# Three dense chunks instead of two, and indirect DMAs tied one by one to TensorE products, in a gated scan followed by a mixture of experts

## Chip, cores and metric

One core of a Trainium2 chip. The time is the device time of one execution in microseconds, median of several runs. The kernel works in float32, apart from a few small helper matrices in bfloat16.

## What is computed

4096 tokens (16 sequences of 256) of 128 channels pass through two residual layers. The first is a gated linear recurrence along each sequence, the second a mixture of 32 experts of which each token uses four.

```python
# layer 1, on layernorm(x)
it = sigmoid(x @ Wi.T + bi);  rt = sigmoid(x @ Wr.T + br)
at = exp(-8.0 * softplus(cap_lambda) * rt)
h  = scan(h = at * h + sqrt(1 - at**2) * (it * x))
x  = x + layernorm(h)
# layer 2, on layernorm(x)
scores  = sigmoid(x @ gate_w.T)
topk    = top_k(scores + e_bias, 4);  weights = scores[topk] / sum
out     = sum over e of weight_e * (silu(x @ w1[e]) * (x @ w3[e])) @ w2[e]     # 128 -> 96 -> 128
x  = x + layernorm(out)
```

## The kernel before

The tokens are cut into eight chunks of 512. Every chunk goes through `mix` (layer 1, router, choice of four experts). Then a chunk takes one of two ways through the experts.

A **dense** chunk (chunks 0 and 7, `DENSE`) computes all 32 experts for all its tokens and multiplies by a combine weight that is zero for experts not chosen. The 32 x 96 = 3072 hidden units are cut into 24 steps (`UB`) of 128. In each step (`dense`), TensorE makes three products, `dg`, `du` (line 990, with w1 and w3) and `dw` (the combine weight spread over the units, bfloat16), ACT applies silu (line 998), DVE multiplies twice (lines 1001 and 1007), and a fourth product (line 1011) adds the step into the accumulator `acc`. `finish` transposes, normalizes and stores the chunk.

A chunk that goes **by token** belongs to a group, `GROUPS`: chunks 1 to 3 and chunks 4 to 6. `send` scatters each token's row four times, once for each chosen expert, into a table in DRAM with a region for each expert: sixteen indirect DMAs a chunk, all from POOL (line 450). When the whole group is sent, `loads` (line 790, SP) brings blocks of 128 rows of one expert back, four blocks at a time, and `experts` runs them: transpose (`xT_ps`, line 806), w1 and w3 together (`gu`, 820), silu and multiply (826, 828), transpose (`aT_ps`, 836), w2 (`y_ps`, 850), and a store to a second table in DRAM (861). A group has `tokens * 4 / 128 + 31` blocks, so that every expert's last block has room: 79 for three chunks. When a group's last block is stored, `fetch` gathers each token's four result rows, again with sixteen indirect DMAs a chunk (line 928), weights and adds them on DVE (936 to 944), and `combine` normalizes, adds the residual and stores.

The order of the instructions on TensorE, DVE, ACT and SP is fixed when the program is built. Each piece of work is a generator that yields the engine that it needs next and a planned cost; `Order.run` plays the pieces against each other by cost, due time and buffer slots, and emits the instructions in that order. A piece that yields `POOL, 1.29 * K` is charged for four indirect DMAs at once. Expert blocks are due early on TensorE, and dense steps late, so that dense steps fill in. POOL issues the indirect DMAs in the order of emission.

`after(ins, others)` makes an instruction wait for other instructions. `apart` declares that the scatters don't collide with each other.

Of the kernel before, what the change touches and what calls it, by code (L numbers as in the profile page):

```python
# [18 lines left out]
P = 128  # L19
EPS = 1e-5  # L20
K = 4
GROUPS = ((1, 2, 3), (4, 5, 6))
DENSE = (0, 7)
MIXES = 6
TILES = 40
HELD = 4
# [2 lines left out]
PE, DVE, ACT, POOL, SP, TIME = "pe", "dve", "act", "pool", "sp", "time"  # L29
# [88 lines left out]
SOON = 0.3  # L118
STAY = 6.0
LEAD, STEP, PACE = 45.0, 20.6, 0.9  # L120
SLOT, UNTIL = "slot", "until"


@with_exitstack
def tile_gated_scan_then_moe(
# [28 lines left out]
    nc = tc.nc  # L154
# [6 lines left out]
    SEQS = CH // T  # L161
    NG = len(GROUPS)
    TG = [CH * len(chunks) for chunks in GROUPS]
    UB = E * I // P
    NB = [t * K // P + E - 1 for t in TG]
    NBM = max(NB)
    QB = 4
    RB = 3
    assert C == P and H == P and CH % T == 0 and E * I % P == 0 and 3 * E <= P
    assert sorted(sum(GROUPS, ()) + DENSE) == list(range(N // CH))  # L170

# [20 lines left out]
    def after(ins, others):  # L192

        for o in others:
            tc.add_manual_dep(
                ins.ins, o.ins.name,
                mybir.DependencyInfo(mybir.DependencyClass.Sync, mybir.DependencyReason.DATA),
                reason="rows in DRAM",
            )
# [225 lines left out]
    def apart(ins, key):  # L425

        tc.declare_no_dep(ins.ins, group=key, reason="rows of their own")
        tc.add_to_no_dep_group(key, ins.ins)
# [7 lines left out]
    def normalize(comb, pool, c):  # L436
# [2 lines left out]
        nc.vector.reciprocal(total, total)  # L439
        nc.vector.tensor_tensor(comb, comb, total.to_broadcast([P, TPC, E]), ALU.mult)  # L440

    def send(g, cg):

        c = GROUPS[g][cg]
        yield UNTIL, lambda: times["rows", c][0] if ("rows", c) in times else None
        _, rows, hn = times["rows", c]
        for j in range(TPC):
            yield POOL, 1.29 * K
            for k in range(K):
                ins = nc.gpsimd.indirect_dma_start(  # L450
                    out=rows_in[g],
                    out_offset=bass.IndirectOffsetOnAxis(ap=rows[:, j, k : k + 1], axis=0),
                    in_=hn[:, j, :], in_offset=None,
                )
                apart(ins, f"in_{g}")
                sent[g].append(ins)
        times["sent", g] = order.now
        yield TIME, 2.5
        give("hn", "w")
# [25 lines left out]
    def mix(c):  # L485

        g = next((g for g in range(NG) if c in GROUPS[g]), None)
        if g is not None:
            cg = GROUPS[g].index(c)
        yield UNTIL, lambda: 0.0 if c < MIXES else times.get(("mixed", c - MIXES))  # L490
# [266 lines left out]
    ended = [0] * NG  # L757
# [36 lines left out]
    def experts(g, q):  # L794

        nb, n_ = min(QB, NB[g] - q), f"{g}_{q}"
        yield UNTIL, lambda: times["xb", g, q][0] if ("xb", g, q) in times else None
        yield UNTIL, lambda: 0.0 if began[g] == q // QB else None
        yield SLOT, "blk", "w", "w", "w"
        began[g] += 1  # L800
        _, xb = times["xb", g, q]
        yield SLOT, "s", "ps"
        yield PE, 0.11 * nb
        pt = bank(f"xT_ps_{n_}")
        for b in range(nb):
            nc.tensor.transpose(pt[:, b * P : (b + 1) * P], xb[:, b, :], ident)  # L806
        give("xb", "w")
        yield ACT, 0.6
        xT = work.tile([P, QB * P], F32, tag="w", name=f"xT_{n_}")
        nc.scalar.copy(xT[:, : nb * P], pt[:, : nb * P])  # L810
        give("s", "ps")
        act = work.tile([P, QB, P], F32, tag="w", name=f"act_{n_}")[:, :, :I]
        for h in range(0, nb, 2):
            m = min(2, nb - h)
            yield SLOT, "s", "ps"
            yield PE, 0.33 * m
            pg = bank(f"gu_{n_}_{h}")[:, : 4 * I].rearrange("p (b f) -> p b f", b=2)
            for b in range(m):
                _, e = regs[g, q + h + b]
                nc.tensor.matmul(  # L820
                    pg[:, b, :], lhsT=xT[:, (h + b) * P : (h + b + 1) * P],
                    rhs=w13[:, :, bass.ds(e, 1), :].rearrange("h s o i -> h s (o i)"),
                    start=True, stop=True,
                )
            yield ACT, 0.33, "silu"
            nc.scalar.activation(act[:, h : h + m, :], pg[:, :m, 0:I], AF.Silu)  # L826
            yield DVE, 0.35
            nc.vector.tensor_tensor(  # L828
                act[:, h : h + m, :], act[:, h : h + m, :], pg[:, :m, I : 2 * I], ALU.mult
            )  # L830
            give("s", "ps")
        yield SLOT, "s", "ps"
        yield PE, 0.11 * nb
        pa = bank(f"aT_ps_{n_}")
        for b in range(nb):
            nc.tensor.transpose(pa[:I, b * P : (b + 1) * P], act[:, b, :], ident)  # L836
        aT = work.tile([P, QB * P], F32, tag="w", name=f"aT_{n_}")[:I]
        if q // QB % 2:
            yield DVE, 0.6
            nc.vector.tensor_copy(aT[:, : nb * P], pa[:I, : nb * P])  # L840
        else:
            yield ACT, 0.6
            nc.scalar.copy(aT[:, : nb * P], pa[:I, : nb * P])  # L843
        give("s", "ps")
        yield SLOT, "s", "ps"
        yield PE, 0.22 * nb
        py = bank(f"y_ps_{n_}").rearrange("p (b h) -> p b h", h=H)
        for b in range(nb):
            _, e = regs[g, q + b]
            nc.tensor.matmul(  # L850
                py[:, b, :], lhsT=aT[:, b * P : (b + 1) * P],
                rhs=w2_sb[:, bass.ds(e, 1), :].rearrange("i o h -> i (o h)"),
                start=True, stop=True,
            )
        yield SLOT, "yb", "w"
        yield ACT, 0.6
        yb = work.tile([P, QB, H], F32, tag="w", name=f"yb_{n_}")
        nc.scalar.copy(yb[:, :nb, :], py[:, :nb, :])  # L858
        give("s", "ps", "blk", "w", "w", "w")
        yield SP, 0.4  # L860
        done[g].append(nc.sync.dma_start(
            out=rows_out[g].rearrange("(i p) h -> p i h", p=P)[:, q : q + nb, :],
            in_=yb[:, :nb, :],
        ))
        ended[g] += 1
        if (q // QB + 1) % RB == 0 or q + QB >= NB[g]:
            give("regs")
        times["done", g] = order.now
        yield TIME, 2.5
        give("yb", "w")  # L870
# [46 lines left out]
    def fetch(g, cg, j):  # L917

        c = GROUPS[g][cg]
        yield UNTIL, lambda: times["done", g] + 2.5 if ended[g] * QB >= NB[g] else None  # L920
        yield UNTIL, lambda: times["slots", c][0] if ("slots", c) in times else None
        yield UNTIL, lambda: 0.0 if fetched[0] == turn[c] * TPC + j else None
        yield SLOT, "yk", "w"
        _, rows, wk = times["slots", c]
        yield POOL, 1.29 * K
        yk = work.tile([P, K, H], F32, tag="w", name=f"yk_{c}_{j}")
        for k in range(K):
            ins = nc.gpsimd.indirect_dma_start(  # L928
                out=yk[:, k, :], out_offset=None, in_=rows_out[g],
                in_offset=bass.IndirectOffsetOnAxis(ap=rows[:, j, k : k + 1], axis=0),  # L930
            )
            after(ins, done[g])
        fetched[0] += 1
        yield TIME, 2.4
        yield DVE, 0.7
        nc.vector.tensor_tensor(
            yk, yk, wk[:, j, :].unsqueeze(2).to_broadcast([P, K, H]), ALU.mult
        )
        yield DVE, 0.7
        nc.vector.tensor_tensor(yk[:, 0:2, :], yk[:, 0:2, :], yk[:, 2:4, :], ALU.add)  # L940
        yield UNTIL, lambda: times["res", c][0] if ("res", c) in times else None
        yield DVE, 0.4
        ff = times["res", c][1]
        nc.vector.tensor_tensor(ff[:, j, :], yk[:, 0, :], yk[:, 1, :], ALU.add)
        give("yk", "w")
        summed[c] = summed.get(c, 0) + 1
        times["summed", c] = order.now
# [19 lines left out]
    accs, acts = {}, {}  # L967
    downs = [0] * len(DENSE)

    def dense(d, k):  # L970

        c = DENSE[d]
        yield UNTIL, lambda: times["hT", c][0] if ("hT", c) in times else None
# [13 lines left out]

        def product(name, lhsT, rhs):
            ps = bank(f"d{name}_{c}_{k}")
            nc.tensor.matmul(ps, lhsT=lhsT, rhs=rhs, start=True, stop=True)  # L990
            return ps

        yield PE, 0.86
# [24 lines left out]
    def finish(d):  # L1018

        c = DENSE[d]  # L1020
        yield UNTIL, lambda: times["down", d] if downs[d] == UB else None
# [31 lines left out]
    for g, chunks in enumerate(GROUPS):  # L1053
# [15 lines left out]
        ]  # L1069
    for d, c in enumerate(DENSE):  # L1070
        pieces += [
# [36 lines left out]
```

## Time and profile before

| what | us |
|---|---|
| median of 3 runs | 440.73 (436.21 to 441.47) |
| the profiled execution's own time | 580.8 |
| its span, first to last instruction | 579.1 |
| mean granted TensorE clock in it | 0.823 of full speed |

| share of the chain that ended last | |
|---|---|
| PE | 48% |
| another core or an unknown queue | 16% |
| DVE | 13% |
| ACT | 11% |
| "issue" (no wait shown) | 11% |

The profile is of one execution, which took 140 us longer than the median of the others. A row of a group of instructions names the line, the engine, the operation, output and inputs, the count, then busy time and the mean of one in ns, and the idle time just before these instructions with what ended it. "remote" and "another core or an unknown queue" stand where the profile does not show who released the waiting engine. In the rows by slices the span is cut into 40 parts of 14.5 us, and each digit is the busy share in tenths.

### The profile page before, as it was taken

How to read it: one execution, taken by the hardware profiler on the slowest of the kernel's cores; microseconds unless marked ns; L12 is line 12 of the kernel's file. 1: busy time of each engine (PE TensorE's matmuls, PEld its weight loads, DVE VectorE, ACT ScalarE, POOL GpSimd, SP SyncE). 2: the span in 40 equal slices, each digit the busy share in tenths (PEclk: the TensorE clock that was granted, in tenths of full speed). 3: DMA queues.
4: the chain of work that ended last, by engine and by line, in shares of the span. 5: the costliest groups of instructions: out<-in, count | busy, mean ns of one | idle time of the engine just before them, and what ended most of it. 6: DMA issues, size and time to landing. Idle time of an engine off the chain costs nothing.

```text
span 579.1 us, 6527 instructions
## 1 busy us (share of the span) xinstructions
PE 368.5 (64%) x1555; PEld 236.8 (41%) x1555; DVE 313.5 (54%) x1185; ACT 251.6 (43%) x473; POOL 202.9 (35%) x227
## 2 busy tenths in 40 slices
PE   0345766767883982588559863288799993235940
PEld 0123342332432871477447542266678631012410
DVE  6956692839482763287218640257577451013785
ACT  1599895659421741666235311144355520001321
POOL 9200046643645017100720077236400077771000
PEclk9986767779698887699759985599899998666995
DMA  8245535100131133223222432044544212110001
GB/s 236 66 133 140 139 91 152 41 32 25 50 100 64 55 101 100 73 70 109 91 70 59 119 109 71 25 120 132 146 118 139 88 45 54 53 51 14 18 1 54
DMA packets 82068, 48.57 MB, mean 84 GB/s; under 512 B 15696, under 2 KB 78960, under 8 KB 82032
## 3 DMA queue, kind: packets, MB, share of 16 engines
q1 hardware_dynamic: 74976, 35.40, 21.6%
q0 software_dynamic: 6144, 12.60, 7.5%
q10 hardware_dynamic: 912, 0.17, 0.2%
q8 instruction: 13, 0.21, 0.1%
q14 instruction: 23, 0.19, 0.1%
HBM read 25.20 MB, written 22.94 MB: 83 GB/s over the span
## 4 chain that ended last, share of the span: by engine, by line
PE 48%; another core or an unknown queue 16%; DVE 13%; ACT 11%; issue 11%; DMA 1%; ACTq 0%; DVEq 0%
PE gu L820 9%; PE acc L1011 8%; PE y_ps L850 7%; PE dg L990 6%; PE du L990 6%; PE aT_ps L836 3%; PE xT_ps L806 2%; PE pl L569 2%; PE dw L990 1%; PE pi L510 1%; PE pr L510 1%; ACT h L395 1%; DVE nt_a L375 1%; DVE st_a L471 1%
## 5 line engine op out<-in xcount | busy, mean ns | idle before, releaser
L450 POOL DMA_INDIRECT rows_in<-hn,rows x96 | 92.7, 965 | 184.3 <-DVE x_all L551 60.6
L928 POOL DMA_INDIRECT yk<-rows_out,slots x96 | 93.1, 970 | 135.4 <-PE dw L990 50.1
L820 PE MATMUL gu<-w,xT 128*128 x316 | 71.3, 360 | 36.9 <-ACT xT L810 19.0
L1011 PE MATMUL acc<-a,w_all 128*128 128x512 f32 x96 | 58.4, 698 | 48.2 <-DVE a L1007 28.5
L820 PEld LDWEIGHTS gu<-w,xT 128*128 128x128 f32 x316 | 56.8, 210 | 45.9 <-issue 23.3
L998 ACT ACTIVATE a<-dg 128x512 f32<-128x512 f32 x48 | 28.6, 598 | 92.8 <-remote 38.6
L1007 DVE TENSOR_TENSOR a<-a,dw 128x512 f32<-128x512 f32 x48 | 32.4, 684 | 64.3 <-remote 34.9
L850 PE MATMUL y_ps<-w_sb,aT 96*128 x316 | 48.7, 305 | 26.2 <-ACT aT L843 11.3
L828 DVE TENSOR_TENSOR act<-act,gu 128x192 f32<-128x192 f32 x80 | 27.0, 346 | 67.9 <-ACT act L826 53.1
L850 PEld LDWEIGHTS y_ps<-w_sb,aT 96*128 96x128 f32 x316 | 43.8, 212 | 39.9 <-ACT aT L843 16.3
L826 ACT ACTIVATE act<-gu 128x192 f32<-128x192 f32 x80 | 25.7, 330 | 68.7 <-PE gu L820 29.7
L990 PE MATMUL dg<-hT,w 128*128 128x512 f32 x96 | 55.4, 662 | 0.0
L990 PE MATMUL du<-hT,w 128*128 128x512 f32 x96 | 50.9, 612 | 0.0
L858 ACT COPY yb<-y_ps 128x512 f32<-128x512 f32 (+1 forms) x40 | 23.1, 581 | 52.5 <-PE y_ps L850 23.4
L1001 DVE TENSOR_TENSOR a<-a,du 128x512 f32<-128x512 f32 x48 | 32.4, 681 | 23.6 <-issue 7.4
L1011 PEld LDWEIGHTS acc<-a,w_all 128*128 128x128 f32 x96 | 17.0, 211 | 67.9 <-DVE a L1007 40.3
L810 ACT COPY xT<-xT_ps 128x512 f32<-128x512 f32 (+1 forms) x40 | 22.8, 582 | 33.5 <-remote 23.8
L836 PE MATMUL aT_ps<-ident,act 128*96 128x128 f32 x158 | 25.6, 287 | 11.1 <-issue 7.4
L990 PEld LDWEIGHTS dg<-hT,w 128*128 128x128 f32 x96 | 20.2, 217 | 19.0 <-issue 17.6
L836 PEld LDWEIGHTS aT_ps<-ident,act 128*96 128x96 f32 x158 | 18.5, 132 | 19.4 <-issue 15.5
L806 PE MATMUL xT_ps<-ident,xb 128*128 128x128 f32 x158 | 25.4, 297 | 0.4 <-DVE lists L749 0.4
L990 PEld LDWEIGHTS du<-hT,w 128*128 128x128 f32 x96 | 18.7, 205 | 14.6 <-issue 13.0
(205 smaller groups left out, 590.2 us busy)
## 6 DMA issues: line engine op xcount, KB each, us to landing
xb<-rows_in SPq DMA_DIRECT2D x158, 64.0 KB
rows_out<-yb SPq DMA_DIRECT2D x38, 256.0 KB
rows_in<-zeros SPq DMA_DIRECT2D x8, 512.0 KB
w<-in_L_ffn_w_dram SPq DMA_DIRECT2D x8, 384.0 KB
x_all<-in_L_attn_x_dram SPq DMA_DIRECT2D x8, 256.0 KB
w_all<-in_L_ffn_w_dram SPq DMA_DIRECT2D x4, 384.0 KB
w_sb<-in_L_ffn_w_dram SPq DMA_DIRECT2D x4, 384.0 KB
rows_in<-hn,rows POOLq DMA_INDIRECT x96
```

The source lines that it names most:

```text
L450: ins = nc.gpsimd.indirect_dma_start(out=rows_in[g], out_offset=bass.IndirectOffsetOnAxis(ap=rows[:, j, k : k + 1], axis=0), in_=hn[:, j, ...
L806: nc.tensor.transpose(pt[:, b * P : (b + 1) * P], xb[:, b, :], ident)
L820: nc.tensor.matmul(pg[:, b, :], lhsT=xT[:, (h + b) * P : (h + b + 1) * P], rhs=w13[:, :, bass.ds(e, 1), :].rearrange("h s o i -> h s (o i) ...
L828: nc.vector.tensor_tensor(act[:, h : h + m, :], act[:, h : h + m, :], pg[:, :m, I : 2 * I], ALU.mult)
L836: nc.tensor.transpose(pa[:I, b * P : (b + 1) * P], act[:, b, :], ident)
L850: nc.tensor.matmul(py[:, b, :], lhsT=aT[:, b * P : (b + 1) * P], rhs=w2_sb[:, bass.ds(e, 1), :].rearrange("i o h -> i (o h)"), start=True, ...
L928: ins = nc.gpsimd.indirect_dma_start(out=yk[:, k, :], out_offset=None, in_=rows_out[g], in_offset=bass.IndirectOffsetOnAxis(ap=rows[:, j, ...
L990: nc.tensor.matmul(ps, lhsT=lhsT, rhs=rhs, start=True, stop=True)
L998: nc.scalar.activation(a, pg, AF.Silu)
L1001: nc.vector.tensor_tensor(a, a, pu, ALU.mult)
L1007: nc.vector.tensor_tensor(a, a, pw, ALU.mult)
L1011: nc.tensor.matmul(accs[d], lhsT=w2_all[:, k, :], rhs=a, start=(k == 0), stop=(k == UB - 1))
```

## The change

The second group becomes chunks 4 and 5, and chunk 6 joins the dense chunks. The planner charges each indirect DMA by itself, at `RATE` = 1.9 instead of four at once at 1.29 each. And each indirect DMA waits for the last `y_ps`, `dg`, `du` or `dw` product that was emitted before it (`beat`). A gather is spaced and made to wait in this way only while dense steps or expert blocks are left to emit (`left`); after that it is charged 1.26 and waits as before. The `acc` product is not recorded in `beat`.

```diff
-GROUPS = ((1, 2, 3), (4, 5, 6))
-DENSE = (0, 7)
+GROUPS = ((1,2,3),(4,5))
+DENSE = (0,6,7)
...
+RATE = 1.9
...
+    beat = [None]
+
+    def in_pace(ins):
+
+        if beat[0] is not None:
+            after(ins, beat)
+
+    def left():
+
+        return sum(downs) < len(DENSE) * UB or any(ended[g] * QB < NB[g] for g in range(NG))
...
         for j in range(TPC):
-            yield POOL, 1.29 * K
             for k in range(K):
+                yield POOL, RATE
                 ins = nc.gpsimd.indirect_dma_start(
...
                 apart(ins, f"in_{g}")
+                in_pace(ins)
                 sent[g].append(ins)
...
-            nc.tensor.matmul(
+            beat[0] = nc.tensor.matmul(
                 py[:, b, :], lhsT=aT[:, b * P : (b + 1) * P],
...
-        yield POOL, 1.29 * K
         yk = work.tile([P, K, H], F32, tag="w", name=f"yk_{c}_{j}")
         for k in range(K):
+            yield POOL, RATE if left() else 1.26
             ins = nc.gpsimd.indirect_dma_start(
...
             after(ins, done[g])
+            if left():
+                in_pace(ins)
...
-            nc.tensor.matmul(ps, lhsT=lhsT, rhs=rhs, start=True, stop=True)
+            beat[0] = nc.tensor.matmul(ps, lhsT=lhsT, rhs=rhs, start=True, stop=True)
```

## The prediction

> **What bounds the kernel now.** I read the header and the rows by slices first, then the groups of instructions, then a table of three stretches, then the timeline inside a run of indirect DMAs and inside an undisturbed stretch.
>
> ```profile
> span 579.1 us, 6527 instructions
> PE 368.5 (64%) x1555; PEld 236.8 (41%) x1555; DVE 313.5 (54%) x1185; ACT 251.6 (43%) x473; POOL 202.9 (35%) x227
> ...
> PE   0345766767883982588559863288799993235940
> ...
> POOL 9200046643645017100720077236400077771000
> PEclk9986767779698887699759985599899998666995
> ...
> L450 POOL DMA_INDIRECT rows_in<-hn,rows x96 | 92.7, 965 | 184.3 <-DVE x_all L551 60.6
> L928 POOL DMA_INDIRECT yk<-rows_out,slots x96 | 93.1, 970 | 135.4 <-PE dw L990 50.1
> ```
>
> TensorE is busiest. It falls to 2 and 3 tenths where POOL stands at 6 to 7 tenths (slices 23 and 24, 34 to 36), and the granted clock falls with it. The 192 indirect DMAs are POOL's only work after the start.
>
> ```profile
> 28.00:172.00 144.00, 98.13 (x282) 49.74 (x283) 92.37 (x417) 105.04 (x169) 51.93 (x54) 0.77 0.32 90
> 172.00:460.00 288.00, 204.68 (x1135) 161.78 (x1134) 146.91 (x524) 118.78 (x253) 88.11 (x91) 0.85 0.32 93
> 460.00:579.00 119.00, 59.07 (x129) 22.87 (x127) 51.62 (x148) 17.45 (x35) 45.72 (x48) 0.77 0.14 37
> ```
>
> The columns are the stretch, its length, busy time of PE, PEld, DVE, ACT and POOL, then clock, DMA share and GB/s. I cut at the first block of an expert (172) and after the last one (460). Stage one is mixing, with ACT busy 105 of 144 us. Stage two is experts with dense steps between them. Stage three is the last 48 gathers beside the rest of the dense steps, and PE works only half of it. Why, the timeline of stage three shows:
>
> ```profile
> 504.92 0.94 POOL L928 DMA_INDIRECT yk<-rows_out,slots  x1 [0.30 <-issue]
> 505.17 0.60 ACT L998 ACTIVATE a<-dg 128x512 f32<-128x512 f32 x1 [18.37 <-remote]
> 506.17 0.95 POOL L928 DMA_INDIRECT yk<-rows_out,slots  x1 [0.30 <-issue]
> ...
> 509.31 0.69 DVE L1007 TENSOR_TENSOR a<-a,dw 128x512 f32<-128x512 f32 x1 [13.38 <-remote]
> ```
>
> The indirect DMAs go every 1.25 us without a gap, while ACT and DVE sit 18.37 and 13.38 us for products that PE had started by 493.95; the releaser is unknown. From 463.4 to 523.5 PE is idle 32 us by the timeline. Runs of four DMAs (5 us, around 390 and 396) show next to no such idleness. So the stall is real in this execution and belongs to long runs: PE's idle time inside runs after 165, beyond a normal tenth, comes to about 75 us; stage two and three also lose some 35 us to matmuls at the lower clock (busy time times one minus clock).
>
> **How this execution stands to the timed runs.** It took 580.8 us (span 579.1 and 1.7 around it); the median of three runs is 440.73. [...] Here it is 140 us. [...] 580.8 less about 110 us of stalls and clock leaves 471, still above 440.73. A timed run has room for few of them. I take the measurement, and this decides the sign.
>
> **What the change costs in dense steps.** One more chunk keeps all experts: 24 more steps (72 for 48). The undisturbed end gives the price:
>
> ```profile
> 550.33 1.12 PE L1011 MATMUL acc<-a,w_all 128*128 128x512 f32 x2
> ...
> 552.37 1.02 PE L990 MATMUL du<-hT,w 128*128 128x512 f32 x2
> ...
> 553.31 1.13 PE L1011 MATMUL acc<-a,w_all 128*128 128x512 f32 x2
> ```
>
> Start to start 2.98 us at full clock (where dg, du, acc and dw follow one another with no wait, 538.70 to 541.49, it is 2.79). So 24 x 2.98 = +71.5 us of PE. DVE gets 24 x (0.681 + 0.684) = 32.8 us and ACT 24 x 0.598 = 14.4, which lie under the step's 2.98 us of PE.
>
> **What it saves in blocks.** The second group loses a chunk: 512 tokens x 4 / 128 = 16 blocks (63 for 79). A block costs:
>
> ```profile
> 446.69 1.06 PE L850 MATMUL y_ps<-w_sb,aT 96*128 x8
> ...
> 447.58 0.82 PE L820 MATMUL gu<-w,xT 128*128 x4
> ...
> 449.00 1.02 PE L990 MATMUL dg<-hT,w 128*128 128x512 f32 x2
> ...
> 449.86 0.60 PE L836 MATMUL aT_ps<-ident,act 128*96 128x128 f32 x4
> ...
> 450.29 0.82 PE L820 MATMUL gu<-w,xT 128*128 x4
> ```
>
> y: 0.89 us for four blocks, gu about 0.65 for two, aT 0.43 for four, xT as aT: 0.22 + 0.325 + 0.11 + 0.11 = 0.76 us. 16 x 0.76 = -12.2 us of PE. Net on PE: +59. The 16 loads and four stores of those blocks leave SP's queue, and 32 of 192 indirect DMAs leave POOL (32 x 1.26 = 40 us); both engines were waiting, so this counts only where a run of gathers sets the end, below.
>
> **Where it lands.** The static order of the changed program, counted on PE: before the first block 20 dense steps are done (14 before the change), before the last block's product 33 (29), after it 39 (19). With the prices above, PE work up to the last block is about the same in both, 237 against 240 us; between first and last block it is 147 against 171. So the added work lies behind the last block.
>
> Stage three before, without stalls: first gather 3.7 us after the last product, 48 x 1.25 = 60.0, about 2 to land (assumed; no row), and 10.3 from the last yk multiply (568.75) to the end (579.1): 76 us. It covered its 19 dense steps (57 us). After: 39 x 2.98 = 116.2, and 11.6 from the last acc (555.44) to the end of a dense chunk (DVE's final add is at 562.91, the output as behind the last one): 128 us, or 120 at 2.79 a step. The 32 gathers, now spaced at the planner's 1.9 us, take 61 and hide. [...] Stage three: **+44 to +52**, taken +50.
>
> Stage one: each scatter now waits for the latest product emitted before it, so a chunk's 16 take about 16 x 1.9 = 30 us for 20. Behind the waiting scatter stand all later ones on POOL; the block loads on SP wait for the group's last. The third chunk's scatters began at 137.5 and ended at 157.5; now 168 to 170. **+11**; bounds: 0 if the products are done anyway, +30 if they lag. PE fills part of it with six more dense steps, which are already taken off stage three.
>
> Stage two: PE needs 24 us less. A timed run has about 440.7 - 165 - 76 = 200 us there for 171 of PE work (165 estimated from the 172 less the 5 to 7 us of stalls seen in stage one): 86%. At the same share 147 us takes 171, **-29**; at 92%, because the few real stalls go, 160, **-40**. Taken -34.
>
> Sum on the timed run: 440.7 + 11 - 34 + 50 = **468 us**. On the profiled execution: 580.8 + 11, less about 115 in stage two (stalls, clock, blocks), + 9 in stage three (128 for 119): about 485. So the profile should improve by far more than 50 us while the timed runs get slower.
>
> **Rivals.**
> Faster: the timed runs do lose time at long runs of indirect DMAs, only less than the profiled one. For: the link of run length to idleness. Against: the sum above. With 60 us of such losses removed, 468 becomes 408; PE's full-rate work (345) plus 28 us before it starts and 12 behind it make 385 a floor. It decides from about 45 us of losses. 405 to 431.
> No change: stage one ends earlier than I think (150 instead of 165), so stage two holds idleness that tighter spacing removes: 15 more us gained, and the scatter delay does not show: 468 - 15 - 11 = 442.
> Much slower: the waits on products lag the plan; the scatters of each chunk take 2.9 us apiece, the first block comes 30 us later, and dense chunk 0 has no steps left to cover it: about 490.
> The spacing may also do nothing, when products are always done before POOL asks. Then the profile keeps its stalls and the timed run lacks the 11 us and some of the 34: about 463, inside my own range.
>
> **Chances.** Forecast 0.69 (450 to 485), no change 0.15 (432 to 449), faster 0.11, much slower 0.05. A measurement of this kernel tells about 2% from no change (432 to 450). Faster 0.11, same 0.15, slower 0.74. The likeliest is 468; the range 441 to 488 leaves out the faster case and part of the last.
>
> **What the changed profile would show.** 72 steps in L990's groups; 142 blocks; the stretch behind the last y_ps about 128 us with PE over 90% busy at full clock; indirect DMAs 1.9 us or more apart, and no "remote" waits of 10 us. I am wrong if the stretch behind the last block is below 100 us, if it comes before 300 in a run as fast as the timed one, or if the timed runs drop along with the profiled one.

## The result, and the profile after

Timed side by side on one chip, the changed kernel took 484.43 us (median of 4 runs), the kernel before 439.39: a ratio of 1.104 (95% interval 1.096 to 1.113), slower. The profiled execution of the changed kernel has a span of 482.7 us.

The page of the changed kernel, its header and its rows by slices (12.1 us each):

```profile
span 482.7 us, 6679 instructions
PE 393.4 (81%) x1627; PEld 233.2 (48%) x1627; DVE 332.0 (69%) x1194; ACT 258.4 (54%) x481; POOL 172.6 (36%) x195
...
PE   1344475889798979899798888889999999998991
...
POOL 9400003455446464454100013544544545443100
PEclk9966775999789999999899999999999999998996
```

TensorE now works in 7 to 9 tenths of every slice after the first quarter but the last, and mostly at 9 tenths of its clock (0.932 in the mean). POOL never fills a slice by more than 6 tenths after the start. The holes of before are gone from the profile, and yet the timed result is 45 us worse.

Every expert block starts with its transpose (`xT_ps`) and ends with its last product (`y_ps`). In the changed kernel (duration min/median/max in ns, then first and last start in us):

```profile
L819 PE MATMUL xT_ps<-ident,xb x142: 270/273/333, 177.3 to 346.1; 128*128 128x128 f32 x142
...
L863 PE MATMUL y_ps<-w_sb,aT x284: 272/275/422, 186.6 to 355.6; 96*128 x142
```

Three stretches of it, from 28 us on, cut at the first block of an expert and after the last one (columns: stretch, length, busy time of PE, PEld, DVE, ACT, POOL, clock, DMA share, GB/s):

```profile
28.00:177.00 149.00, 113.17 (x354) 54.19 (x355) 113.94 (x504) 115.14 (x186) 51.96 (x53) 0.84 0.29 83
177.00:356.00 179.00, 160.28 (x989) 130.08 (x988) 108.39 (x365) 100.15 (x215) 58.73 (x61) 0.98 0.44 126
356.00:482.00 126.00, 113.56 (x277) 46.51 (x275) 86.85 (x230) 32.52 (x65) 44.71 (x47) 0.96 0.15 40
```

Stage three is 127 us long (to the end of the span) with PE busy 90% of it, against 119 us half idle in the profile of before. Part of the changed kernel's timeline in that stage:

```profile
424.67 1.02 PE L1005 MATMUL du<-hT,w 128*128 128x512 f32 x2
...
425.96 0.94 POOL L941 DMA_INDIRECT yk<-rows_out,slots  x1 [0.99 <-PE du L1005]
...
427.65 0.38 PE L1005 MATMUL dw<-combT,spread 96*128 96x512 bf16 x1
...
428.08 0.94 POOL L941 DMA_INDIRECT yk<-rows_out,slots  x1 [1.18 <-PE dw L1005]
...
429.33 0.94 POOL L941 DMA_INDIRECT yk<-rows_out,slots  x1 [0.30 <-issue]
```

POOL sits idle about 1 us for a dense product before most of these gathers, though not all: two still start 1.25 us apart at 428.08 and 429.33. The 47 gathers behind the last block start between 358.7 and 448.5, 1.95 us apart on average. TensorE is the bound, and the gathers hide under it.

One thing stays open at this point: before took 440 us when timed and 580.8 when profiled.

### The profile page after: what moved, and what is told of

Same layout as the page of the kernel before. It is cut to its first block, busy times and chain, and to the rows that moved or that the text cites. A ratio compares the mean times of both kernels' runs of the same rounds, so it can differ in the third digit from the quotient of the medians.

```text
span 482.7 us, 6679 instructions
## 1 busy us (share of the span) xinstructions
PE 393.4 (81%) x1627; PEld 233.2 (48%) x1627; DVE 332.0 (69%) x1194; ACT 258.4 (54%) x481; POOL 172.6 (36%) x195
## 4 chain that ended last, share of the span: by engine, by line
PE 44%; DVE 3%; issue 2%; ACT 2%; ACTq 0%; DVEq 0%
PE acc L1026 9%; PE du L1005 8%; PE dg L1005 8%; PE gu L833 6%; PE y_ps L863 5%; PE aT_ps L849 2%; PE dw L1005 2%; PE xT_ps L819 2%; ACT res L396 0%; DVE aT L853 0%; DVE a L1022 0%; DVE st_d L386 0%; ACT L1013 0%; ACT L588 0%; ACT yb L871 0%
## 5 line engine op out<-in xcount | busy, mean ns | idle before, releaser
L462 POOL DMA_INDIRECT rows_in<-hn,rows x80 | 78.5, 982 | 139.0 <-ACT xn L511 61.6
L941 POOL DMA_INDIRECT yk<-rows_out,slots x80 | 76.8, 961 | 137.1 <-DMA rows_out<-yb 51.1
L1026 PE MATMUL acc<-a,w_all 128*128 128x512 f32 x144 | 79.3, 642 | 8.3 <-DVE a L1022 8.2
L1005 PE MATMUL du<-hT,w 128*128 128x512 f32 x144 | 75.3, 605 | 0.4 <-ACT xT L823 0.4
L1005 PE MATMUL dg<-hT,w 128*128 128x512 f32 x144 | 74.8, 601 | 0.0
L1022 DVE TENSOR_TENSOR a<-a,dw 128x512 f32<-128x512 f32 x72 | 48.8, 685 | 29.9 <-PE dw L1005 29.5
L833 PE MATMUL gu<-w,xT 128*128 x284 | 56.7, 334 | 11.0 <-issue 6.0
L1016 DVE TENSOR_TENSOR a<-a,du 128x512 f32<-128x512 f32 x72 | 48.4, 682 | 24.8 <-PE du L1005 12.7
L1005 PE MATMUL dw<-combT,spread 96*128 96x512 bf16 x72 | 27.5, 397 | 0.4 <-ACT a L1013 0.4
L523 PE MATMUL pi<-xnT,wiT 128*128 128x512 f32 x16 | 13.5, 941 | 15.3 <-ACT xnT L411 15.2
```

The source lines that it names most:

```text
L462: ins = nc.gpsimd.indirect_dma_start(out=rows_in[g], out_offset=bass.IndirectOffsetOnAxis(ap=rows[:, j, k : k + 1], axis=0), in_=hn[:, j, ...
L833: nc.tensor.matmul(pg[:, b, :], lhsT=xT[:, (h + b) * P : (h + b + 1) * P], rhs=w13[:, :, bass.ds(e, 1), :].rearrange("h s o i -> h s (o i) ...
L941: ins = nc.gpsimd.indirect_dma_start(out=yk[:, k, :], out_offset=None, in_=rows_out[g], in_offset=bass.IndirectOffsetOnAxis(ap=rows[:, j, ...
L1005: beat[0] = nc.tensor.matmul(ps, lhsT=lhsT, rhs=rhs, start=True, stop=True)
L1016: nc.vector.tensor_tensor(a, a, pu, ALU.mult)
L1022: nc.vector.tensor_tensor(a, a, pw, ALU.mult)
```

## Experiments

The runs fell on several chips. Each was timed beside the kernel before on the same chip, and that time is given with it. **Quiet** chips are those where before took about 440 us, **stalling** chips those where it took about 580. Each chip was met once, so a chip and its condition at that hour can't be told apart here.

### The parts alone: groups, pacing, charge, and the last gathers

Edits: `e1_groups_only` is before with the new groups.

```diff
-GROUPS = ((1, 2, 3), (4, 5, 6))
-DENSE = (0, 7)
+GROUPS = ((1,2,3),(4,5))
+DENSE = (0,6,7)
```

> Three dense chunks and groups of three and two, indirect DMAs as before (no waits on products, charged four at once). The static order has 42 dense steps after the last block (39 in the changed kernel, 19 before). Theory (timed runs hold few burst stalls, the added dense steps behind the last block are the whole price): timed 475 to 492, within 2% of the changed kernel, while the profiled execution is again 70 to 110 us longer than the timed ones. Rival (timed runs lose time at long runs of indirect DMAs, and the pacing wins some of it back): timed 500 or more.

`e2_pace_only` is the changed kernel with the old groups:

```diff
-GROUPS = ((1,2,3),(4,5))
-DENSE = (0,6,7)
+GROUPS = ((1, 2, 3), (4, 5, 6))
+DENSE = (0, 7)
```

> The groups of before (3 and 3, two dense chunks), every indirect DMA charged 1.9 and tied to the last product. 35 dense steps before the last block, 13 after. Theory: stage one about 11 us later, stage two 15 us more of TensorE work, the last 48 gathers at 1.9 us while dense steps last (39 us) and then at 1.26: about 90 us behind the last block; timed 438 to 455, same or slightly slower than before, and the profiled execution within 10 us of the timed ones. Rival (timed runs stall at long runs too): timed below 420.

`e3_charge_only` takes the waits out of that again:

```diff
     def in_pace(ins):
 
-        if beat[0] is not None:
-            after(ins, beat)
+        return
```

> As e2_pace_only with the same static order on every engine, but no indirect DMA waits for a product. Theory: timed within 2% of e2_pace_only, a few us faster since the scatters of a chunk take 20 us again instead of 30; the profiled execution 80 us or more above the timed ones, because the runs are long again. Rival (the wait itself wins time in timed runs): 10 us or more slower than e2_pace_only.

`e4_no_last_gathers` is before without the second group's `fetch` and `combine`, so it leaves out the results of chunks 4 to 6:

```diff
-            (read + STEP * (cg + 1), combine(g, cg)) for cg in range(len(chunks))
+            (read + STEP * (cg + 1), combine(g, cg)) for cg in range(len(chunks)) if g == 0
...
-            for cg in range(len(chunks)) for j in range(TPC)
+            for cg in range(len(chunks)) for j in range(TPC) if g == 0
```

> The kernel before without the gathers, weighting, normalization and stores of chunks 4 to 6 (their outputs are left out); same order on TensorE. Theory: a timed stage three before is 76 us, bound by the 48 gathers, and 19 dense steps and the end of a dense chunk take 68 without them: timed 428 to 436. Rival (the stalls of stage three, 43 us in the profiled execution, stand in timed runs): 405 or less.

Measured on one quiet chip, before at 440.02 us:

| kernel | us | ratio to before (95%) | span profiled |
|---|---|---|---|
| groups only | 483.75 | 1.101 (1.094 to 1.109) | 482.2 |
| pacing only | 479.15 | 1.091 (1.083 to 1.098) | 477.7 |
| charge only, no waits | 469.56 | 1.065 (1.056 to 1.074) | 467.9 |
| no last gathers | 424.87 | 0.965 (0.956 to 0.974) | 427.9 (an execution of 429.55) |

The first row says that the regrouping alone is enough for the whole loss: 483.75 is the changed kernel's time. But the other half of its expectation failed. The profiled execution was to be 70 to 110 us longer than the timed ones, and it is as long as they are. Its 32 last gathers follow one another every 1.25 us or so (354.3 to 394.2), and nothing stalls. Three windows of 20 us of `e1_groups_only`, the first two inside that run, the last almost all behind it:

```profile
352.00:372.00 20.00, 20.00 (x50) 8.43 (x50) 16.31 (x43) 5.42 (x11) 13.47 (x14) 1.00 0.24 66
372.00:392.00 20.00, 19.93 (x49) 7.93 (x47) 15.45 (x40) 5.50 (x11) 15.10 (x17) 1.00 0.26 66
392.00:412.00 20.00, 20.00 (x50) 8.60 (x50) 14.99 (x42) 5.29 (x11) 1.88 (x2) 1.00 0.04 11
```

PE is busy all the time, whether or not POOL is. So profiling by itself does not cause the stalls, and long runs of indirect DMAs don't stall everywhere.

Pacing alone was expected at 438 to 455 and took 479. The charge alone, which only changes the order that the planner writes, took 470: 29.5 of the 39 us. Its first block also comes as late as that of pacing alone (179.9 and 179.4). The waits on top add 9.6, all behind the last block (88 us from there to the end against 78). Why the charge costs so much, the loads of the experts' blocks show. In `e3_charge_only`, with the window from the first load to the first block below them:

```profile
L802 SPq DMA_DIRECT2D xb<-rows_in x158: 332/333/1468, 144.0 to 372.5; - x158
...
L818 PE MATMUL xT_ps<-ident,xb x158: 270/273/473, 179.9 to 381.9; 128*128 128x128 f32 x158
...
144.00:180.00 36.00, 31.15 (x95) 13.75 (x94) 32.18 (x129) 15.56 (x25) 24.45 (x25) 1.00 0.29 88
```

The first block is loaded at 144.0 and TensorE takes it at 179.9, after 36 us in which it is busy with other products for 31. The load isn't late: the block's place in the fixed order is late. A scatter that is charged 1.9 us instead of 1.29 makes the planner expect the blocks later. It puts six more dense steps ahead of them (20 instead of 14, 18 us at 2.98 each) and more of the later chunks' mixing. That pushes every block back. With two dense chunks nothing is gained for it later, since the 48 last gathers still take their time: 78 us from the last block to the end, with 13 dense steps there instead of 19.

Without the last gathers, stage three was to shrink by 8 us; before got faster by 15. The gathers do set the end of before, by more than I had worked out. This kernel also shows where the blocks of before lie on a quiet chip, since its order on TensorE is that of before up to the last of them:

```profile
L806 PE MATMUL xT_ps<-ident,xb x158: 270/273/328, 153.3 to 352.4; 128*128 128x128 f32 x158
...
L850 PE MATMUL y_ps<-w_sb,aT x316: 270/275/578, 161.6 to 362.6; 96*128 x158
```

### Where the 580 us come from

`e5_before_again` is before with no edit. `e6_half_chunk` is the changed kernel with only 12 of the 24 steps of chunk 6:

```diff
     downs = [0] * len(DENSE)
+    STEPS = [UB, UB // 2, UB]
...
-            accs[d], lhsT=w2_all[:, k, :], rhs=a, start=(k == 0), stop=(k == UB - 1)
+            accs[d], lhsT=w2_all[:, k, :], rhs=a, start=(k == 0), stop=(k == STEPS[d] - 1)
```

(and `STEPS` for `UB` where a chunk's steps are made and counted). `e7_wait_only` keeps the waits and takes the old charge, with the old groups; `e8_four_and_two` is before with other groups:

```diff
-RATE = 1.9
+RATE = 1.29
...
-GROUPS = ((1, 2, 3), (4, 5, 6))
+GROUPS = ((1, 2, 3, 4), (5, 6))
```

> The kernel before, unchanged, profiled once more. Two kernels with the same long runs of indirect DMAs (e1_groups_only, e3_charge_only) had profiled executions as long as their timed ones. Theory: the first profile of before was one disturbed execution, and this one has a span of 435 to 445, first block at about 152, last block product at about 362. Rival (profiling this program stalls at its long runs): again 540 or more.

> The changed kernel with only the first 12 of the 24 steps of the middle dense chunk (chunk 6; its other 48 x 32 hidden units are left out). Same order before the last block, 27 dense steps after it instead of 39. Theory (the added steps are serial work behind the last block, 2.98 us each): 484.4 - 36 = 449, 446 to 453. Rival (gathers or DVE set that stage): above 460.

> The groups of before, each indirect DMA tied to the last product, but charged 1.29: the order on TensorE is exactly that of before, so that the waits alone are added. Theory (it was the planner's charge that moved the first block by 27 us, since e2_pace_only and e3_charge_only both begin it at 180; the waits cost only behind the last block, about 10 us there): first block 152 to 160, timed 440 to 452. Rival (the waits hold the scatters): first block 170 or later, timed 460 or more.

> The kernel before with groups of four and two chunks (same 158 blocks, same 48 dense steps). The last group gathers 32 times, not 48: 40 us + 16 = 56, so the 18 dense steps left there set the end: 65 us instead of 76. The first block comes later (19 dense steps before it instead of 14: about 178), with less TensorE work between first and last block (156 against 171, about 180 us). Theory: timed 418 to 432, faster. Rival (the first group's longer wait leaves TensorE idle in stage one): 440 or more.

These four met a stalling chip. Before took 576.8 to 584.0 us there in seven timed runs, and 577.8 in the profiled execution of `e5_before_again`. So the 580 us are neither one disturbed execution, as I had expected, nor the profiler: they come with the chip, or with its condition at that time, run after run. Three windows of `e5_before_again` (busy PE, clock, DMA share, GB/s), the second and third inside the last 48 gathers:

```profile
460.00:480.00 20.00, 17.57 (x42) 1.00 0.18 46
480.00:500.00 20.00, 5.93 (x11) 0.76 0.18 49
500.00:520.00 20.00, 5.63 (x7) 0.59 0.20 53
```

Set these beside the windows of `e1_groups_only`: there, on another chip, with gathers and dense steps of the same kind, PE is busy 20 us in 20, and here it falls under 6. In the timeline of `e5_before_again`, the waits of ACT and DVE for finished products are back:

```profile
489.33 1.56 PE L990 MATMUL dg<-hT,w 128*128 128x512 f32 x2
...
490.73 0.38 PE L990 MATMUL dw<-combT,spread 96*128 96x512 bf16 x1
...
490.94 1.02 PE L990 MATMUL du<-hT,w 128*128 128x512 f32 x2
...
501.46 0.60 ACT L998 ACTIVATE a<-dg 128x512 f32<-128x512 f32 x1 [15.51 <-remote]
...
504.92 0.69 DVE L1007 TENSOR_TENSOR a<-a,dw 128x512 f32<-128x512 f32 x1 [12.66 <-remote]
...
505.66 2.07 PE L1011 MATMUL acc<-a,w_all 128*128 128x512 f32 x2 [13.69 <-issue]
```

Paired step by step, ACT takes the `dg` product 10.6 us after its end and DVE the `dw` product 13.8 us after its end, and TensorE's next product starts only then, at 505.66.

On this chip the waits alone (`e7_wait_only`) took 485.31 us, 0.833 of before (0.829 to 0.838). Its order on TensorE, ACT and DVE is that of before, so here breaking up the runs is what saves 96 us. Its first block came at 157.9, as expected; the 440 to 452 us expected for it were meant for a chip without stalls. Groups of four and two, with long runs, took 591.41 (1.016); whether they are faster without stalls, as expected, no run shows. The half chunk took 458.32, expected 446 to 453: of the 36 us of steps taken out, 26 came back (the changed kernel at its 484.43 on another chip). Its dense steps were done early enough that the last gathers set the end instead, 99.5 us behind the last block where 27 steps and a chunk's end make 92. Its last gather starts at 440.8, 85 us behind the last block: with 47 gathers there, the room under the dense steps is small.

### The changed kernel on a stalling chip, and the two open columns

`e9_after_again` and `e10_four_and_two_again` are the changed kernel and `e8_four_and_two` with no further edit; `e11_groups_only_again` and `e12_wait_only_again` are `e1_groups_only` and `e7_wait_only`.

> The changed kernel, unchanged, beside before on one more chip. On one chip before took 440 us and kernels with long runs of indirect DMAs had no stalls; on the next before took 581. Theory (the stalls behind long runs belong to a chip, not to the profiler, and short runs avoid them): on a chip where before takes about 580, the changed kernel takes 484 to 495, a ratio near 0.84; on a chip where before takes 440, it takes 484 and the ratio is 1.10. Rival (the slow chip is slower for every kernel): 600 or more where before takes 580.

> The kernel before with groups of four and two chunks, as e8_four_and_two, which took 591 beside 581 for before. Theory: on a chip without stalls 418 to 432, faster than before, since stage three is 65 us instead of 76; on a chip with stalls about 590 again. Rival (the later first block costs more than that): 440 or more where before takes 440.

> Three dense chunks without any pacing, as e1_groups_only (484 beside 440 for before). Theory (chips differ in whether long runs of indirect DMAs hold the other engines up): beside a before of about 580, this takes 560 or more, since its 160 indirect DMAs again go in runs of 16 and 32, while its twin with pacing took 487; beside a before of 440, 484 again. Rival (on the chip with stalls the regrouping, not the pacing, made the changed kernel fast): about 490 beside a before of 580.

> The groups and the order of before, with each indirect DMA tied to the last product, as e7_wait_only (485 beside 581 for before). Theory: beside a before of 440 the waits cost 0 to 12 us, 440 to 452, which would make it the version that does well on both kinds of chip; beside a before of about 580, 485 again. Rival (the waits hold the scatters on any chip): 460 or more beside a before of 440.

The first pair met another stalling chip (before 586.54 us), the second a quiet one (before 440.82).

| kernel | quiet chip, us (before) | stalling chip, us (before) |
|---|---|---|
| changed kernel | 484.43 (439.39) | 486.65 (586.54), ratio 0.832 (0.826 to 0.838) |
| groups only | 483.75 (440.02), 484.92 (440.82) | not run |
| waits only | 445.01 (440.82), ratio 1.011 (1.002 to 1.020) | 485.31 (581.5), ratio 0.833 |
| groups of four and two | not run | 591.41 (581.5), 604.35 (586.54) |

The changed kernel takes 484 on a quiet chip and 487 on a stalling one. Before takes 440 and 587. The change is 10% slower on the one and 17% faster on the other.

`e12_wait_only_again` has before's order on TensorE exactly, so its stages on a quiet chip stand in for those of before, of which there is no quiet profile (the first block and the last product lie within 0.3 us of those in `e4_no_last_gathers`, which has before's own indirect DMAs up to there):

```profile
0.00:153.60 153.60, 98.50 (x294) 47.86 (x295) 115.10 (x515) 115.01 (x186) 68.61 (x88) 0.86 0.39 109
153.60:363.70 210.10, 187.25 (x1135) 148.29 (x1134) 147.15 (x523) 119.14 (x253) 90.86 (x91) 0.98 0.46 130
363.70:443.40 79.70, 53.23 (x129) 20.91 (x127) 52.20 (x148) 17.46 (x35) 46.59 (x48) 0.87 0.21 56
```

Its first block is loaded at 148.2 and taken at 153.6:

```profile
L803 SPq DMA_DIRECT2D xb<-rows_in x158: 332/333/1701, 148.2 to 349.4; - x158
...
L819 PE MATMUL xT_ps<-ident,xb x158: 270/273/329, 153.6 to 352.6; 128*128 128x128 f32 x158
```

So with the waits, but without the charge, the first block is not held up: it is the charge that moves stage one. The same program on the stalling chip (`e7_wait_only`) still loses 40 us:

```profile
0.00:158.00 158.00, 98.97 (x294) 48.08 (x295) 114.74 (x509) 115.11 (x186) 70.01 (x89) 0.86 0.37 104
158.00:394.50 236.50, 195.88 (x1135) 152.82 (x1134) 147.06 (x529) 118.77 (x253) 90.12 (x91) 0.94 0.41 117
394.50:484.00 89.50, 56.03 (x129) 21.58 (x127) 51.80 (x148) 17.50 (x35) 46.05 (x48) 0.79 0.18 50
```

Stage two is 26 us longer and stage three 10, at a lower clock. The changed kernel loses only 2 us there. Counting indirect DMAs at most 1.6 us apart as one stretch, its longest on the stalling chip was 9.2 us, in `e7_wait_only` 17.2; in the profile of before it is 60.0, the last 48 gathers. That the shorter stretches make the difference is likely but not shown, since the groups differ too.

No version run here beats both kernels on both kinds of chip. The waits alone come closest: within about 1% of before where nothing stalls, level with the changed kernel where it does (485 and 487).

## Why the prediction came out as it did

It forecast slower, 468 us within 441 to 488, and the changed kernel took 484. Its sum had three terms, which can now be read off as differences between the profiles of the changed kernel and of `e12_wait_only_again`, both without stalls.

- **Dense steps behind the last block**: forecast +50 us with 128 us in all. Measured 126.8 against 79.7, **+47**. The 39 steps and the price of 2.98 us a step, from the undisturbed end of the profile of before (granted clock 1.00 from 550.0 to 555.5), held. That the gathers hide under it held too, with less room than worked out: 47 of them lie behind the last block, not 32, because 15 of the first group's come late as well, and they take 91 us instead of 61.
- **Stage two**: forecast -34. Measured 178.6 against 210.1, **-31**.
- **Stage one**: forecast +11, for scatters that wait. Measured 177.3 against 153.6, **+24**, and for another reason: `e3_charge_only`, with no waits, shows the same late first block (179.9), and `e12_wait_only_again`, with waits, does not (153.6). The mis-sized term is this one. The group's scatters did end at 168.4, as forecast (168 to 170). But in `e3_charge_only` they end at 142.6 and the first block is no earlier. The six extra dense steps were counted as work moved out of stage three, which they are, but not as a delay in front of every block. Stage one of before was also shorter than I took it (153.6, not 165), and stage two longer (210, not 200).

24 - 31 + 47 = 40, and before itself is 4 us faster than its stand-in: 44 to 45, as measured. Those 4 us lie in stage three: a run of before of 440.02 us has a span of 438.3, and with the last block ending at 362.9 (`e4_no_last_gathers`) that leaves 75 us, where the prediction had worked out 76 (with 2 us assumed for a gather to land; in the changed kernel the median of 80 gathers is 2.6).

The sign and two of the three terms were right for their stated reasons. That 484 falls inside the range owes something to its width: it lies 16 us from 468 and 6 us from the 490 of the much slower rival.

One step failed as reasoning though it did not turn the sign. I put the 140 us between profile and timed runs down to the profiled execution, which no run had shown. Every later profiled execution lies within 5 us of the median of the runs timed beside it, 484.37 and 484.43 for the changed kernel, and its span is 1.7 us shorter. So the profile and the timed runs of before most likely came from different chips; the record does not name the chips of these first runs. One small sum there is off as well: busy time times one minus the clock, an estimate from 204.68 us at 0.85 and 59.07 us at 0.77, gives 44 us for stages two and three, not 35, which leaves 462 instead of 471, still above 440.73.

Taken for what it was, the profile described a stalling chip, and the forecast that it should fall to about 485 came true there: 485.5 in the span of `e9_after_again`. The terms came true too. Against the profile of before, stage one is 7 us longer (forecast 11), stage two 106 shorter (115) and stage three 6 longer (9). The rival that the timed runs do stall was given 0.11 and 405 to 431. It is wrong for the quiet chips, where no stall shows, and on stalling chips its sign is right: before loses some 140 us and the changed kernel almost none of it.

The rival of no change was right that stage one of before ends early (150, measured 153), but not that stage two would win more from it: it got 31 us shorter, where that rival needed 49.

The rival of much slower waits had the first block 30 us late, which is nearly what came (24), but not for its reason. On quiet chips the waits cost 4 us with the old order and charge and 9.6 with the new charge. Next to the regrouping, charge and waits together cost nothing, since the changed kernel and `e1_groups_only` take the same time. There the late first block is paid back: stage one is 26 us longer (177.3 against 151.2), stage two 21 shorter and stage three 5, probably because three dense chunks leave TensorE full to the end wherever a step stands (in stage three PE is busy 113.6 of 126 us in the changed kernel, 119.1 of 131 in `e1_groups_only`). With two chunks the same delay was a loss of 30.

## What to carry to other kernels

When a profiled execution and the timed runs of one program lie far apart, find out first whether they come from the same chip; if they don't, the profile answers for one kind of chip only, and a change that breaks up a stall can be a gain on one and a loss on the other. Where a planner writes the order, a changed cost estimate moves instructions that it doesn't name: read the new place of the first dependent work, not only the new wait. To break up runs on one queue, this kernel could tie them to products that are issued anyway and leave the planner's charge alone: that cost 1% where nothing stalled and saved 17% where before stalled.

## What the hardware showed

On two of the four chips identified in these runs the kernel before, whose last 48 gathers start without a gap, took 576.8 to 588.2 us, on the other two 434.7 to 443.7: 14 timed runs on each kind, with no overlap. On a stalling chip ACT sat idle for 15.51 us and DVE for 12.66, though the products that they waited for had ended 10.6 and 13.8 us before, while POOL went on issuing every 1.25 us (`e5_before_again`). On a quiet chip PE was busy 39.9 us of 40 under 31 gathers in a row (`e1_groups_only`). With no stretch over 9.2 us, the changed kernel took 487 on a stalling chip, against 484 on a quiet one. What differs between the chips, whether it lasts, and which path carries the delay, was not settled. Not tried: the regrouping without pacing on a stalling chip, so what pacing is worth in the changed groups there; and groups of four and two on a quiet one.
